# An LSTM with residual: the last 38 time steps with the hidden units in two halves

## The chip, the cores and the metric

The kernel runs on one core of a Trainium2 chip. A core has a matrix engine (TensorE, PE in the profile, with its weight loads as PEld), VectorE (DVE), ScalarE (ACT), GpSimd (POOL) and SyncE (SP), which here issues nearly all DMAs. The metric is the device time of one execution in microseconds, as the median of several runs.

## The reference, cut to what matters

```python
def lstm_forward(x, h0, Wx, Wh, b):            # x 32 x 512 x 512, all float32
    Hd = h0.shape[1]                           # 512
    xW = jnp.einsum('ntd,dg->ntg', x, Wx) + b  # Wx, Wh: 512 x 2048
    c0 = jnp.zeros_like(h0)
    def step(carry, xw_t):
        prev_h, prev_c = carry
        a = xw_t + prev_h @ Wh
        i = jax.nn.sigmoid(a[:, :Hd])
        f = jax.nn.sigmoid(a[:, Hd:2 * Hd])
        o = jax.nn.sigmoid(a[:, 2 * Hd:3 * Hd])
        g = jnp.tanh(a[:, 3 * Hd:])
        next_c = f * prev_c + i * g
        next_h = o * jnp.tanh(next_c)
        return ((next_h, next_c), next_h)
    (_, _), hs = jax.lax.scan(step, (h0, c0), jnp.swapaxes(xW, 0, 1))
    return jnp.swapaxes(hs, 0, 1)
return x + lstm_forward(x, cond_1024, L0_cond_Wx, L0_cond_Wh, L0_cond_b)
```

There are 32 sequences of 512 steps. Each step needs the h of the step before, so the 512 products h Wh come one after the other; the product x Wx has no such order.

## The kernel before, in words

**Layout.** The 128 partitions hold four groups j of 32 sequences: group j holds units 128 j to 128 j + 127 of each gate, and the 512 free columns are the four gates (i, f, g, o) of 128 units each. Every matmul has 32 stationary columns and writes 32 partitions, so that four of them, for the four j, use the array side by side. All is float32, and the profile shows each matmul as two.

**The loop.** The loop over k does one time step: `h_part(k)`, then the products of a *window* v = k + 4, then `cell(k)`. `h_part` (L667 to L678) adds h Wh to two PSUM banks that ScalarE has filled with the step's x Wx + b ("seeds", `seed_first` and `seed_last`, L656 to L662): first the 384 columns of i, f and g into bank `gates[t % 2]`, then the 128 columns of o into the other one. Consecutive steps so swap the banks. `cell` (L684 to L717) does two sigmoids, two tanhs, the sums and products on VectorE, and a transpose of 32 x 32 blocks that makes h the stationary operand `ht` of the next step. GpSimd adds x to it for the output (L710) and adds the bias to the x Wx of a coming step (L652).

**x Wx.** The first 40 steps and the last 16 (the tail, from END = 496) are multiplied plainly or nearly so. The 456 between them go by a fast matrix algorithm with 20 products per super-block of 24 steps, spread over the windows; a planner with due times (`push`, `run_due`) puts its sums on VectorE, its results go to DRAM and come back as `xw` two or three steps ahead. Each product of the fast algorithm occupies PE in windows w to w + 4 and is read out until w + 5; the last product of the last super-block begins at window 475.

**The tail's plain products.** `tail_products(v)` (L629 to L644) starts at window `FIRST_TAIL` = 481, which is step 477. From there on every window does two of 64 *pieces* (t, q): a quarter of the depth of one tail step's x Wx, all 512 columns, in 16 matmul rows. When the four pieces of a step are done, VectorE adds the bias (`keep_direct`, L620) into a free buffer (`tail_rooms`) that stays until its step seeds it. The six PSUM banks of the fast algorithm serve in turn (`tail_bank`). Two blocks of Wx, overwritten earlier, are loaded again into `raw_again` (L778 to L781, at windows 476 and 478).

**What sets the order.** Each engine runs its instructions in the program's order, which is written out by hand as above. All DMAs of this part stand in SP's queue in program order too, so a transfer that waits holds those behind it.

Of the kernel before, what the change touches and what calls it, by code (L numbers as in the profile page):

```python
# [9 lines left out]
F32 = mybir.dt.float32  # L10
AF = mybir.ActivationFunctionType
# [3 lines left out]
P = 128  # L15
B = 32
T = 512
NJ = 4
G = 4
IFG = 3 * P  # L20
ROW = 8
# [95 lines left out]
def begin(n):  # L117

    return 6 * (n // 5) + n % 5


class Job:
# [4 lines left out]
def kernel(  # L127
# [9 lines left out]
    nc = tc.nc  # L137
# [486 lines left out]
    tail_rooms, whole = [], []  # L624

    def tail_bank(t):
        return (*pps, *accs, p5)[t % 6]

    def tail_products(v):  # L629
        if v == FIRST_TAIL:  # L630
            tail_rooms.extend(node.rearrange("p t e b -> p (t e b)") for node in node_free)
            for f in free[: (TAIL - len(tail_rooms) + 1) // 2]:
                tail_rooms.extend([f[:, 0], f[:, 1]])
            assert len(tail_rooms) >= TAIL
        if v < FIRST_TAIL:
# [8 lines left out]
        del pieces[:2]  # L644

    def load_xw(t):
        xw[t] = upool.tile([P, G * P], F32, name=f"xw_{t}", tag="xw", bufs=4)
# [5 lines left out]

    def seed_first(t):  # L656
        if t < T:
            nc.scalar.copy(gates[t % 2][:, 0:IFG], xw[t][:, 0:IFG])  # L658

    def seed_last(t):  # L660
        if t < T:
# [5 lines left out]
    def h_part(t):  # L667
        for g, cols in ((gates[t % 2], slice(0, IFG)), (gates[(t + 1) % 2], slice(IFG, G * P))):
            for k in range(NJ):
                for j in range(NJ):  # L670
                    nc.tensor.matmul(  # L671
                        g[j * B : (j + 1) * B, cols],
                        state["ht"][:, k, :],
                        wh_sb[:, k, j, cols],
                        start=False,
                        stop=True,
                        skip_group_check=True,
                    )  # L678

    def x_last():  # L680
        state["x"] = work.tile([P, P], F32, name="x_last")
# [2 lines left out]
    def cell(t):  # L684
        n, tt = divmod(t, ROW)
        s = work.tile([P, G, P], F32, name=f"s_{t}", tag="s")
        fc = work.tile([P, P], F32, name=f"fc_{t}", tag="fc")
        c = work.tile([P, P], F32, name=f"c_{t}", tag="c", bufs=2)
        tc_t, h = ig, fc
        ht = work.tile([P, NJ, B], F32, name=f"ht_{t}", tag="ht", bufs=3)  # L690

        g = gates[t % 2].rearrange("p (g u) -> p g u", u=P)
        o = gates[(t + 1) % 2].rearrange("p (g u) -> p g u", u=P)[:, 3]
        nc.scalar.activation(s[:, 0:2], g[:, 0:2], AF.Sigmoid)  # L694
        nc.scalar.activation(s[:, 2], g[:, 2], AF.Tanh)
        nc.scalar.activation(s[:, 3], o, AF.Sigmoid)  # L696
        nc.vector.tensor_mul(fc, s[:, 1], state["c"])  # L697
        nc.vector.tensor_mul(ig, s[:, 0], s[:, 2])  # L698
        nc.vector.tensor_add(c, fc, ig)  # L699
        nc.scalar.activation(tc_t, c, AF.Tanh)  # L700
        nc.vector.tensor_mul(h, s[:, 3], tc_t)  # L701
        if t == T - 1:
            nc.vector.tensor_add(tc_t, h, state["x"])
            nc.sync.dma_start(out=out[n][:, tt * P : (tt + 1) * P], in_=tc_t)
            return
        nc.vector.transpose(ht.rearrange("p q b -> p (q b)"), h)  # L706
        state["c"], state["ht"] = c, ht
        if tt % 2 == 0:
            state["oc"] = opool.tile([P, 2, NJ, B], F32, name=f"oc_{t}", tag="oc")
        (nc.gpsimd if t < T - 3 else nc.vector).tensor_add(state["oc"][:, tt % 2], xr[t][:, tt % 2], ht)  # L710
# [55 lines left out]
    def fetch(v):  # L766

        job = jobs.get(v + 2)
        if job and job.w >= START and len(B_OF[job.kind[1]]) > 1:
            job.ring = [rpool.tile([P, 3, C], F32, name=f"wa_{job.w}", tag="wa", bufs=3), None]  # L770
            nc.sync.dma_start(out=job.ring[0].rearrange("p n c -> p (n c)"), in_=kept[job.kind[1]][0])
        job = jobs.get(v)
        if job and job.w >= START and len(B_OF[job.kind[1]]) > 1:
            job.ring[1] = rpool.tile([P, 4, C], F32, name=f"wb_{job.w}", tag="wb", bufs=4)
            nc.sync.dma_start(out=job.ring[1].rearrange("p n c -> p (n c)"), in_=kept[job.kind[1]][1])
        if v in (FIRST_TAIL - 10, FIRST_TAIL - 8):
            load_row(END // ROW + (v - FIRST_TAIL + 10) // 2)
        if v in (FIRST_TAIL - 5, FIRST_TAIL - 3):  # L778
            i = [i for i in range(8) if i not in single][(v - FIRST_TAIL + 5) // 2]
            raw[i] = rpool.tile([P, 4, C], F32, name=f"raw_again_{i}", tag="wb", bufs=4)  # L780
            nc.sync.dma_start(out=raw[i].rearrange("p n c -> p (n c)"), in_=wx[i])  # L781
        sb, rest = divmod(v + 6 - START, PER)
        if v + 6 in UNIT_AT[2 * NJ :: NJ]:
            load_row(3 + UNIT_AT[2 * NJ :: NJ].index(v + 6))
        if rest < MO and 0 <= sb < NSB:
            load_row(HEAD // ROW + MO * sb + (0, 2, 1)[rest])

    with tc.manual_schedule():
# [45 lines left out]
        for k in range(T):  # L834
            if k % 2 == 0 and k + 2 < T:
                load_residual(k + 2)
            if 2 * 4 - 3 <= k and k + 3 < END:
                load_xw(k + 3)
            h_part(k)
            if 2 * 4 - 2 <= k and k + 2 < END:  # L840
                add_bias(k + 2)
            for m, v in enumerate(windows_of(k)):
                if v == START:
                    assert len(due) == 0 or due[0][0] >= START
                    free.extend(t.rearrange("p (h n) c -> p h (n c)", h=2) for t in others)
                    free.extend(spool.tile([P, 2, 2 * C], F32, name=f"slot_h{i}", tag="sums", bufs=2) for i in range(2))
                announce(v)
                room = ROOM if v >= START - 4 else HEAD_ROOM
                run_due(v, room - evacuate(v, room))
                products(v)  # L850
                tail_products(v)
                fetch(v)
                if k == T - 2:
                    x_last()
                if m == 0:
                    cell(k)
                    seed_first(k + 2)
                    seed_last(k + 1)
                for op in prepare(v + 1):
                    op()  # L860
# [52 lines left out]
```

## Time and profile before

| | |
|---|---|
| median of 3 runs | 3124.21 us (3122.48 to 3124.5) |
| the profiled execution | 3124.46 us, span 3122.6 us |
| granted clock, mean | 0.999 |
| PE busy | 3108.1 us, 100% of the span |
| DVE, ACT, POOL busy | 2253.4, 1606.1, 1068.6 us |
| h Wh on PE (L671) | 32704 matmul rows, mean 380 ns |

The profile is one execution on the chip. A row of a timeline gives the start (us from the span's start), the time, the engine, the line of the kernel, the operation, and out<-in with shapes; rows of one kind that follow each other closely are merged (x64), and in brackets stands the engine's idle time before it with what ended it. The end of a matmul is modelled and rows overlap, so the pace of PE is read from start to start. A row of a group has the busy time, the mean ns of one, and the idle time before it. The chain of waits follows the work back from the last instruction.

### The profile page before, as it was taken

What the parts mean: (1) busy time and instruction counts of PE and PEld (TensorE: products, weight loads), DVE (VectorE), ACT (ScalarE), POOL (GpSimd) and SP (SyncE); (2) the same over time, 40 slices, a digit from 0 to 9 for tenths busy, and PEclk for the clock granted to TensorE, in tenths of its full rate; (3) what the DMA queues carried; (4) which work ended last, traced back from release to release, by engine and by line L of the source; (5) the groups of instructions that cost most, each with busy time, mean ns of one, the idle gap of its engine ahead of it and who ended that gap; (6) DMA issues with size and microseconds to landing.
All of it is one profiled execution on the core that took longest, in us unless ns stands there. A gap on an engine that the chain in (4) does not pass through costs nothing.

```text
span 3122.6 us, 133354 instructions
## 1 busy us (share of the span) xinstructions
PE 3108.1 (100%) x56632; PEld 2022.5 (65%) x56632; DVE 2253.4 (72%) x6107; ACT 1606.1 (51%) x4842; POOL 1068.6 (34%) x1001
## 2 busy tenths in 40 slices
PE   9999999999999999999999999999999999999999
PEld 5666666666666666666666666666666666666554
DVE  6557777777777777777777777777777777777533
ACT  2455555555555555555555555555555555555433
POOL 0223333333333333333333333333333333333320
PEclk9999999999999999999999999999999999999999
DMA  6656666767575766657676757667576767576410
GB/s 246 212 161 209 211 220 189 232 206 234 193 239 174 240 205 207 228 189 231 201 230 205 232 178 234 201 217 231 186 230 197 231 205 237 177 234 202 155 56 26
DMA packets 316084, 631.63 MB, mean 202 GB/s; under 512 B 41952, under 2 KB 107744, under 8 KB 314976
## 3 DMA queue, kind: packets, MB, share of 16 engines
q1 hardware_dynamic: 315344, 623.09, 61.7%
q8 instruction: 446, 7.31, 1.0%
q14 instruction: 150, 1.23, 0.1%
q10 hardware_dynamic: 144, 0.01, 0.0%
HBM read 448.60 MB, written 174.33 MB: 199 GB/s over the span
## 4 chain that ended last, share of the span: by engine, by line
PE 99%; DVE 0%; ACT 0%; DMA 0%; issue 0%; SPq 0%; DVEq 0%
PE gates L671 57%; PE acc L413 17%; PE pp L413 17%; PE p L413 6%; PE pp L604 1%; PE gates L604 1%; PE acc L604 1%; PE p L604 0%; DMA raw_sb<-in_L_cond_Wx_dram 0%; DVE ig L698 0%; DVE c L699 0%; ACT s L694 0%; ACT ig L700 0%; DVE fc L701 0%; DVE fc L697 0%
## 5 line engine op out<-in xcount | busy, mean ns | idle before, releaser
L671 PE MATMUL gates<-wh_sb,ht 128*32 128x384 f32 x32704 | 1873.6, 380 | 7.9 <-DVE ht L706 7.8
L671 PEld LDWEIGHTS gates<-wh_sb,ht 128*32 128x32 f32 x32704 | 1131.9, 110 | 770.9 <-issue 667.2
L710 POOL TENSOR_TENSOR oc<-xr,ht 128x128 f32<-128x128 f32 x509 | 445.2, 875 | 1925.3 <-DVE ht L706 1908.2
L652 POOL TENSOR_TENSOR xw<-xw,bias_sb 128x512 f32<-128x512 f32 x488 | 638.3, 1308 | 110.6 <-DMA xw<-xw 66.6
L694 ACT ACTIVATE s<-gates 128x256 f32<-128x256 f32 x512 | 197.4, 386 | 785.6 <-PE gates L671 785.6
L697 DVE TENSOR_TENSOR fc<-s,c 128x128 f32<-128x128 f32 x511 | 154.0, 301 | 482.7 <-ACT s L694 482.4
L455 ACT COPY pp<-pu 128x512 f32<-128x512 f32 x396 | 237.0, 599 | 153.5 <-DVE slot L563 81.3
L701 DVE TENSOR_TENSOR fc<-s,ig 128x128 f32<-128x128 f32 x512 | 150.4, 294 | 192.6 <-ACT ig L700 192.6
L413 PE MATMUL pp<-wb,node 128*32 128x256 f32 x3040 | 243.9, 379 | 0.0
L696 ACT ACTIVATE s<-gates 128x128 f32<-128x128 f32 x512 | 142.3, 278 | 183.8 <-PE gates L671 183.6
L658 ACT COPY gates<-xw 128x384 f32<-128x384 f32 x492 | 232.7, 473 | 5.9 <-DVE node L620 4.6
L706 DVE STREAM_TRANSPOSE ht<-fc 128x128 f32<-128x128 f32 x511 | 159.1, 311 | 53.4
L456 ACT COPY pp<-acc 128x256 f32<-128x256 f32 x396 | 142.1, 359 | 97.3 <-DVE slot L563 42.0
L700 ACT ACTIVATE ig<-c 128x128 f32<-128x128 f32 x512 | 158.7, 310 | 64.5 <-DVE c L699 31.8
L457 DVE TENSOR_TENSOR pp<-acc,p 128x256 f32<-128x256 f32 x396 | 167.7, 423 | 32.8 <-ACT pp L456 31.0
L449 DVE TENSOR_TENSOR pu<-acc,p 128x256 f32<-128x256 f32 x396 | 163.6, 413 | 25.3 <-ACT p L446 16.4
L446 ACT COPY p<-p 128x256 f32<-128x256 f32 x396 | 149.7, 378 | 48.0 <-PE p L413 42.1
L413 PE MATMUL pp<-wb,s 128*32 128x256 f32 x2128 | 170.8, 379 | 0.0
L413 PE MATMUL acc<-wb,s 128*32 128x256 f32 x2128 | 170.7, 379 | 0.0
L413 PE MATMUL p<-wa,s 128*32 128x256 f32 x2128 | 170.7, 379 | 0.0
L413 PE MATMUL acc<-wa,s 128*32 128x256 f32 x2128 | 170.7, 379 | 0.0
L699 DVE TENSOR_TENSOR c<-fc,ig 128x128 f32<-128x128 f32 x512 | 151.5, 296 | 17.8
(187 smaller groups left out, 4127.9 us busy)
## 6 DMA issues: line engine op xcount, KB each, us to landing
wb<-keep_b SPq DMA_DIRECT2D x266, 512.0 KB, 5.4
xw<-xw SPq DMA_DIRECT2D x488, 256.0 KB, 4.1
wa<-keep_a SPq DMA_DIRECT2D x266, 384.0 KB, 4.6
xw<-slot SPq DMA_DIRECT2D x528, 128.0 KB, 3.3
xr<-in_x_dram SPq DMA_DIRECT2D x256, 128.0 KB, 3.2
out_dram<-oc SPq DMA_DIRECT2D x255, 128.0 KB, 2.6
row<-in_x_dram SPq DMA_DIRECT2D x63, 512.0 KB, 6.2
xw<-slot_h SPq DMA_DIRECT2D x180, 128.0 KB, 3.6
```

The source lines that it names most:

```text
L413: nc.tensor.matmul(dst[t * B : (t + 1) * B], a[:, t], w, start=s in (1, 5) and m == 0, stop=True, skip_group_check=True,)
L449: nc.vector.tensor_add(job.pu[:, 1], job.acc, job.p5)
L455: nc.scalar.copy(job.pp[0], job.pu)
L457: nc.vector.tensor_add(job.pp[1][:, 1], job.acc, job.p5)
L652: nc.gpsimd.tensor_add(xw[t], xw[t], bias_sb)
L658: nc.scalar.copy(gates[t % 2][:, 0:IFG], xw[t][:, 0:IFG])
L671: nc.tensor.matmul(g[j * B : (j + 1) * B, cols], state["ht"][:, k, :], wh_sb[:, k, j, cols], start=False, stop=True, skip_group_check=True,)
L694: nc.scalar.activation(s[:, 0:2], g[:, 0:2], AF.Sigmoid)
L697: nc.vector.tensor_mul(fc, s[:, 1], state["c"])
L700: nc.scalar.activation(tc_t, c, AF.Tanh)
L706: nc.vector.transpose(ht.rearrange("p q b -> p (q b)"), h)
L710: (nc.gpsimd if t < T - 3 else nc.vector).tensor_add(state["oc"][:, tt % 2], xr[t][:, tt % 2], ht)
```

## The change

From step `HALVES` = 474 on (38 steps), the 128 units of each partition group are split into two halves of 64. Half m has its own PSUM bank for all steps, and uses 256 columns of it (four gates of 64 units).

- `h_halves` takes the place of `h_part`: four blocks of two depths k and one half m, in the order (k 0 and 1, half 0), (k 0 and 1, half 1), (k 2 and 3, half 0), (k 2 and 3, half 1). Depths 0 and 1 need only the first half of h, depths 2 and 3 only the second. The moving operand is cut: four runs of 64 columns.
- `cell_halves` does the cell twice, on 64 units each time, first all of half 0 and then all of half 1. The three gate activations of a half are followed by its seed for the next step, into the bank that they have just read.
- The tail's plain products start at window 478 (step 474) in place of 481, with one piece in the first window and two in each later one. Their banks are taken in another order, and a buffer is taken for each tail step when it is needed, in place of all at once.
- The second load of `raw_again` is issued at window 477 in place of 478; the rows of x and the first one stay at their windows.
- The last step adds x to each half and stores both with one DMA. `put_step` is the old end of `cell`, unchanged.

```diff
+LAST = START + PER * (NSB - 1) + begin(R - 1)
+HALVES = LAST + 3 - 4
...
-    FIRST_TAIL = START + PER * (NSB - 1) + begin(R - 1) + 6
-    tail_rooms, whole = [], []
-    def tail_bank(t):
-        return (*pps, *accs, p5)[t % 6]
+    whole = []
+    tail_banks = [p5, accs[1 - LAST % 2], accs[LAST % 2], *pps]
+    def tail_room():
+        if not node_free:
+            f = free.pop(0)
+            return f[:, 0]
+        return node_free.pop(0).rearrange("p t e b -> p (t e b)")
     def tail_products(v):
-        if v == FIRST_TAIL:
-            tail_rooms.extend(node.rearrange("p t e b -> p (t e b)") for node in node_free)
-            for f in free[: (TAIL - len(tail_rooms) + 1) // 2]:
-                tail_rooms.extend([f[:, 0], f[:, 1]])
-            assert len(tail_rooms) >= TAIL
-        if v < FIRST_TAIL:
+        if v < LAST + 3:
             return
         for t in whole:
-            keep_direct(t, tail_bank(t), tail_rooms[t - END])
+            keep_direct(t, tail_banks[(t - END) % 6], tail_room())
         whole.clear()
-        for t, q in pieces[:2]:
-            direct(t, tail_bank(t), (q,))
+        for t, q in pieces[: 1 if v == LAST + 3 else 2]:
+            direct(t, tail_banks[(t - END) % 6], (q,))
...
+    halves = gates[HALVES % 2], gates[(HALVES + 1) % 2]
+    HP = P // 2
+    def half(a, m):
+        return a.rearrange("p (g u) -> p g u", u=P)[:, :, m * HP : (m + 1) * HP]
+    def bank_half(m):
+        return halves[m][:, 0 : G * HP].rearrange("p (g u) -> p g u", u=HP)
+    def seed_half(t, m):
+        if t < T:
+            nc.scalar.copy(bank_half(m), half(xw[t], m))
     def seed_first(t):
-        if t < T:
+        if t == HALVES:
+            seed_half(t, 0)
+        elif t < HALVES:
             nc.scalar.copy(gates[t % 2][:, 0:IFG], xw[t][:, 0:IFG])
...
+    def h_halves(t):
+        for ks in ((0, 1), (2, 3)):
+            for m in range(2):
+                for k in ks:
+                    for j in range(NJ):
+                        nc.tensor.matmul(
+                            bank_half(m)[j * B : (j + 1) * B],
+                            state["ht"][:, k, :],
+                            half(wh_sb[:, k, j], m),
+                            start=False,
+                            stop=True,
+                            skip_group_check=True,
+                        )
...
+    def cell_halves(t):
+        us = [slice(m * HP, (m + 1) * HP) for m in range(2)]
+        def gates_of(m):
+            g, u = bank_half(m), us[m]
+            nc.scalar.activation(s[:, 0:2, u], g[:, 0:2], AF.Sigmoid)
+            nc.scalar.activation(s[:, 2, u], g[:, 2], AF.Tanh)
+            nc.scalar.activation(s[:, 3, u], g[:, 3], AF.Sigmoid)
+        def sums_of(m):
+            u = us[m]
+            nc.vector.tensor_mul(fc[:, u], s[:, 1, u], state["c"][:, u])
+            nc.vector.tensor_mul(ig[:, u], s[:, 0, u], s[:, 2, u])
+            nc.vector.tensor_add(c[:, u], fc[:, u], ig[:, u])
+        def end_of(m):
+            u = us[m]
+            nc.vector.tensor_mul(fc[:, u], s[:, 3, u], ig[:, u])
+            if t == T - 1:
+                nc.vector.tensor_add(ig[:, u], fc[:, u], state["x"][:, u])
+            else:
+                nc.vector.transpose(ht[:, 2 * m : 2 * m + 2].rearrange("p q b -> p (q b)"), fc[:, u])
+        gates_of(0)
+        seed_half(t + 1, 0)
+        sums_of(0)
+        nc.scalar.activation(ig[:, us[0]], c[:, us[0]], AF.Tanh)
+        end_of(0)
+        gates_of(1)
+        seed_half(t + 1, 1)
+        sums_of(1)
+        nc.scalar.activation(ig[:, us[1]], c[:, us[1]], AF.Tanh)
+        end_of(1)
...
-        if v in (FIRST_TAIL - 10, FIRST_TAIL - 8):
-            load_row(END // ROW + (v - FIRST_TAIL + 10) // 2)
-        if v in (FIRST_TAIL - 5, FIRST_TAIL - 3):
+        if v in (LAST - 4, LAST - 2):
+            load_row(END // ROW + (v - LAST + 4) // 2)
+        if v in (LAST + 1, LAST + 2):
...
-            h_part(k)
+            (h_part if k < HALVES else h_halves)(k)
...
-                    cell(k)
+                    (cell if k < HALVES else cell_halves)(k)
```

More of the change, by code (lines that the diff above doesn't have):

```diff
@@ L652, in add_bias @@
         nc.gpsimd.tensor_add(xw[t], xw[t], bias_sb)
+    halves = gates[HALVES % 2], gates[(HALVES + 1) % 2]
[7 more added lines that the diff above has]
+            nc.scalar.copy(bank_half(m), half(xw[t], m))
     def seed_first(t):
-        if t < T:
+        if t == HALVES:
+            seed_half(t, 0)
+        elif t < HALVES:
             nc.scalar.copy(gates[t % 2][:, 0:IFG], xw[t][:, 0:IFG])
     def seed_last(t):
-        if t < T:
+        if t == HALVES:
+            seed_half(t, 1)
+        elif t < HALVES:
             nc.scalar.copy(gates[(t + 1) % 2][:, IFG:], xw[t][:, IFG:])
@@ L701, in cell, with put_step @@
         nc.vector.tensor_mul(h, s[:, 3], tc_t)
[L702 to L705, printed above, removed]
         nc.vector.transpose(ht.rearrange("p q b -> p (q b)"), h)
         state["c"], state["ht"] = c, ht
+        put_step(t)
+    def cell_halves(t):
+        n, tt = divmod(t, ROW)
+        s = work.tile([P, G, P], F32, name=f"s_{t}", tag="s")
+        fc = work.tile([P, P], F32, name=f"fc_{t}", tag="fc")
+        c = work.tile([P, P], F32, name=f"c_{t}", tag="c", bufs=2)
+        ht = work.tile([P, NJ, B], F32, name=f"ht_{t}", tag="ht", bufs=3) if t < T - 1 else None
+        us = [slice(m * HP, (m + 1) * HP) for m in range(2)]
[26 more added lines that the diff above has]
+        end_of(1)
+        if t == T - 1:
+            nc.sync.dma_start(out=out[n][:, tt * P : (tt + 1) * P], in_=ig)
+            return
+        state["c"], state["ht"] = c, ht
+        put_step(t)
+    def put_step(t):
+        n, tt = divmod(t, ROW)
+        ht = state["ht"]
         if tt % 2 == 0:
@@ L775, in fetch @@
             nc.sync.dma_start(out=job.ring[1].rearrange("p n c -> p (n c)"), in_=kept[job.kind[1]][1])
-        if v in (FIRST_TAIL - 10, FIRST_TAIL - 8):
-            load_row(END // ROW + (v - FIRST_TAIL + 10) // 2)
-        if v in (FIRST_TAIL - 5, FIRST_TAIL - 3):
-            i = [i for i in range(8) if i not in single][(v - FIRST_TAIL + 5) // 2]
+        if v in (LAST - 4, LAST - 2):
+            load_row(END // ROW + (v - LAST + 4) // 2)
+        if v in (LAST + 1, LAST + 2):
+            i = [i for i in range(8) if i not in single][v - LAST - 1]
             raw[i] = rpool.tile([P, 4, C], F32, name=f"raw_again_{i}", tag="wb", bufs=4)
```

2 lines of the change are left out of this document (1 added, 1 removed).

## The prediction

> **What bounds the kernel now.** I read the stretches of the last 200 us first, then PE's timeline in them, then one late step on all engines, then Pool. In what follows "step k" is one time step; its h Wh starts with the first L671 of the step.
>
> ```profile
> span 3122.6 us, 133354 instructions
> ...
> 2915.80:2932.70 16.90, 12.73 (x232) 7.37 (x229) 11.01 (x24) 6.31 (x20) 6.93 (x7) 0.99 0.74 221
> 2932.70:2939.50 6.80, 6.80 (x81) 2.81 (x82) 1.39 (x5) 1.79 (x6) 1.71 (x3) 0.78 0.24 77
> 2939.50:3099.10 159.60, 159.56 (x2408) 78.97 (x2408) 52.03 (x165) 53.52 (x180) 33.59 (x47) 1.00 0.16 52
> 3099.10:3122.60 23.50, 16.19 (x272) 8.78 (x271) 7.03 (x24) 6.02 (x21) 0.74 (x2) 1.00 0.08 24
> ```
>
> Columns: stretch, its length, busy time of PE, weight load, DVE, ACT, POOL, then granted clock, DMA share, GB/s. PE lacks 4.2 us of work in the first stretch, runs at a clock of 0.78 in the second, looks full in the third, and idles again in the last. PE's timeline names the steps (474, 475, 476, 477, 478 start with an L671 row each):
>
> ```profile
> 2904.44 3.66 PE L671 MATMUL gates<-wh_sb,ht 128*32 128x384 f32 x64
> 2907.89 0.64 PE L413 MATMUL pp<-wb,node 128*32 128x256 f32 x8
> 2908.32 0.64 PE L413 MATMUL acc<-t,s 128*32 128x256 f32 x8
> ...
> 2915.80 3.66 PE L671 MATMUL gates<-wh_sb,ht 128*32 128x384 f32 x64
> 2920.11 0.64 PE L413 MATMUL pp<-wb,s 128*32 128x256 f32 x8
> 2921.11 3.66 PE L671 MATMUL gates<-wh_sb,ht 128*32 128x384 f32 x64 [0.36 <-DVE ht L706]
> 2924.56 0.64 PE L413 MATMUL pp<-wb,node 128*32 128x256 f32 x8
> 2926.42 3.66 PE L671 MATMUL gates<-wh_sb,ht 128*32 128x384 f32 x64 [1.22 <-DVE ht L706]
> ...
> 2939.50 3.66 PE L671 MATMUL gates<-wh_sb,ht 128*32 128x384 f32 x64
> ```
>
> The first three rows are the price list of a PE that never waits: 3.45 us for h Wh (2904.44 to 2907.89), 0.43 for a group of products. A plain piece is two such groups by length, 0.86. Steps 474 to 477 run out of products, and each next L671 waits for the transposed h. The third stretch looks full but is not. By the chain:
>
> ```profile
> 2932.68 5.16 PE gates L671 x64
> ...
> 2939.55 3.60 PE gates L671 x64
> ...
> 3099.06 3.59 PE gates L671 x64
> ```
>
> Thirty steps, 478 to 508, take 159.51 us, 5.317 each; their work is 3.45 + 2 x 0.86 = 5.17. Step 477 pays 5.16 for what costs 3.60 later. Here is what sets the 5.317:
>
> ```profile
> 2944.84 3.66 PE L671 MATMUL gates<-wh_sb,ht 128*32 128x384 f32 x64
> 2947.68 0.38 ACT L694 ACTIVATE s<-gates 128x256 f32<-128x256 f32 x1 [3.08 <-PE gates L671]
> 2948.10 0.29 DVE L697 TENSOR_TENSOR fc<-s,c 128x128 f32<-128x128 f32 x1 [2.48 <-ACT s L694]
> 2948.31 0.29 DVE L698 TENSOR_TENSOR ig<-s 128x128 f32<-128x128 f32 x1
> 2948.63 0.29 DVE L699 TENSOR_TENSOR c<-fc,ig 128x128 f32<-128x128 f32 x1
> 2948.95 0.31 ACT L700 ACTIVATE ig<-c 128x128 f32<-128x128 f32 x1
> 2949.30 0.29 DVE L701 TENSOR_TENSOR fc<-s,ig 128x128 f32<-128x128 f32 x1 [0.37 <-ACT ig L700]
> 2949.69 0.31 DVE L706 STREAM_TRANSPOSE ht<-fc 128x128 f32<-128x128 f32 x1
> 2950.15 3.66 PE L671 MATMUL gates<-wh_sb,ht 128*32 128x384 f32 x64
> ```
>
> 2.84 us from the start of h Wh to the first activation (the i, f, g columns), then 2.47 us of cell until h is back on PE. Behind the i, f, g columns PE has only the o columns (0.86) and two pieces (1.72), and falls 0.15 short each step. The cell bounds the tail, by a little with products and by nearly 2 us without.
>
> **The change, part by part.** (a) *Half a cell.* The trace has no 64-column instruction; neighbours in size give the slope:
>
> ```profile
> L694 ACT ACTIVATE s<-gates 128x256 f32<-128x256 f32 x512 | 197.4, 386 | 785.6 <-PE gates L671 785.6
> L696 ACT ACTIVATE s<-gates 128x128 f32<-128x128 f32 x512 | 142.3, 278 | 183.8 <-PE gates L671 183.6
> L456 ACT COPY pp<-acc 128x256 f32<-128x256 f32 x396 | 142.1, 359 | 97.3 <-DVE slot L563 42.0
> L457 DVE TENSOR_TENSOR pp<-acc,p 128x256 f32<-128x256 f32 x396 | 167.7, 423 | 32.8 <-ACT pp L456 31.0
> L699 DVE TENSOR_TENSOR c<-fc,ig 128x128 f32<-128x128 f32 x512 | 151.5, 296 | 17.8
> ```
>
> ACT: 0.108 us per 128 columns; DVE: 0.127. So a half saves 0.108 on the two-gate sigmoid, 0.054 on the tanh of c, about 0.064 on each DVE operation. Along the rows of the step above, from activation to PE: 0.42 + 0.21 + 0.32 + 0.32 + 0.35 + 0.39 + 0.46 = 2.47; minus 0.108 + 5 x 0.064 + 0.054 gives **1.99 us** for the first half. Bounds: nothing saved but the 0.108 (2.36), or everything in proportion (1.24); I take the slope, as both engines show one.
>
> The second half follows in the same queues. Its sigmoid stands behind the first half's tanh of c (at 0.97) and starts at 1.12; its DVE operations stand behind the first transpose and start at 1.76; with the same spacings its h is on PE at **3.44 us**. The seeds of the next step move into these queues as well, two copies of 256 columns. The first must end before the first tanh of c is due: sigmoid of o done near 0.52 (estimate, three short activations one behind the other), copy 0.36 by the 256-column row, end 0.91 against 0.97. Six hundredths of slack: a copy that is longer goes straight onto the path.
>
> (b) *h Wh in four blocks of 0.86.* 64 matmuls as before, same columns. The first cell starts after three blocks, 2.84, as now (three of four quarters, as 384 of 512 columns). The built program lets block 1 wait for the first transpose alone and block 3 for the second, and block 2 for its seed (near 2.1). After the first activation PE has block 4 and products: free at 0.86 - 0.27 + 1.72 = 2.31 (0.27: 2.84 less 2.57 of columns). The first h is there at 1.99, the second at 3.44 against 2.31 + 1.72 = 4.03. So with two pieces the step becomes PE's own 5.17. Operands cut into runs of 64 columns are the unknown: no row has one. I take no cost, because eight half-width matmuls (the 0.43 row above) and four full-width ones take the same 0.43 per group, so more beginnings are hidden; the other end is open (first rival).
>
> (c) *Products from step 474.* Their weights must be there:
>
> ```profile
> 2905.83 0.38 SPq L781 DMA_DIRECT2D raw_again<-in_L_cond_Wx_dram  x1
> ...
> 2910.74 1.75 SPq L473 DMA_DIRECT2D xw<-slot_h  x4
> ...
> 2923.03 0.37 SPq L781 DMA_DIRECT2D raw_again<-in_L_cond_Wx_dram  x1
> ```
>
> The first load is issued 14.7 us before the first piece (2920.5, below). The second moves one window up on SP, ahead of an output, a residual row, a load of xw and two groups of stores, to the end of the stores of 2910.74, near 2912.5, and is wanted at 2926; what it passes is issued 0.5 us later, and what stood behind it 0.5 earlier. DVE takes one bias addition for every four pieces, as before, now behind the second transpose, where it is idle; in front of a first half its 0.69 us would come onto the path.
>
> The sum, against the profiled execution (3124.46 us with 3122.6 span; the median is 3124.21):
>
> Steps 474 to 477: before 2915.80 to 2939.50, 23.70. After: 474 is 3.45 + 3 x 0.43 + 0.86 = 5.60; 475 is 3.45 + 0.43 + 1.72 = 5.60; 476 and 477 are 5.17: 21.54. **Gain 2.16**, and seven pieces are done instead of two.
> Steps 478 to 505: 28 x (5.317 - 5.17). **Gain 4.1.**
> Step 506 has one piece, 507 to 511 none. From the start of 506 to the next start and on, the cell bounds: 2.84 + 1.99 = 4.83. Before, 506 starts at 2939.55 + 28 x 5.317 = 3088.43 and the last cell at 3117.77 (below): 29.34. After: 5 x 4.83 + 2.84 = 26.99. **Gain 2.35.**
>
> ```profile
> 3117.77 0.39 ACT L694 ACTIVATE s<-gates 128x256 f32<-128x256 f32 x1 [3.56 <-PE gates L671]
> 3119.71 0.29 DVE L703 TENSOR_TENSOR ig<-fc,x_last 128x128 f32<-128x128 f32 x1
> ```
>
> Last cell: 2.23 us before. After, the second half ends it: addition of x at about 2.88, done 3.1. **Loss 0.87**; the output DMA is the same.
> Together 2.16 + 4.1 + 2.35 - 0.87 = 7.74: **3116.7 us**, 0.25% less.
>
> [...] The second stretch lost about 1.5 us to the clock (6.8 x 0.22), and PE's longest idle time before it is 2.59 us. [...] By the row the loss goes with the gaps; were the slow step another thing and to stay, the sum would be 3118.2, the third rival's case.
>
> **The rivals.** *1. The cut operand slows PE (slower).* Each of 38 steps reads Wh in runs of 64. At 0.20 us a step (7.74 / 38), 6% of 3.45, the gain is gone; at 15% (0.52 us) the time is 3136.4. For it: no row excludes it. Against it: the two equal 0.43 groups.
>
> *2. Pool holds the cell.*
>
> ```profile
> 2930.03 1.27 POOL L652 TENSOR_TENSOR xw<-xw,bias_sb 128x512 f32<-128x512 f32 x1 [3.21 <-DMA xw<-xw]
> 2930.21 1.24 DVE L699 TENSOR_TENSOR c<-fc,ig 128x128 f32<-128x128 f32 x1
> 2944.77 0.46 POOL L710 TENSOR_TENSOR oc<-xr,ht 128x128 f32<-128x128 f32 x1 [3.66 <-DVE ht L706]
> 2945.19 1.28 POOL L652 TENSOR_TENSOR xw<-xw,bias_sb 128x512 f32<-128x512 f32 x1
> ```
>
> The DVE addition that began inside Pool's bias addition took 0.95 us more. [...] Until step 493 Pool adds out and bias behind the whole transposed h, 1.70 us from the start of the one to the end of the other, so from about 3.4 to 5.1 after; the next half cell's first DVE operation is at 5.17 + 0.31 = 5.48. It misses by under 0.4 us. If Pool comes later than that, a hold of 0.95 less the 0.32 that PE has in hand (1.99 against 2.31) is 0.63 in each of 20 steps: 3129.3.
>
> *3. The first steps stay unfilled*, because a hold or a store's wait keeps the clock or the 2 us: 3118 to 3119.
>
> *4. Halves cost more than the slope says.* With nothing saved but the 0.108 the first h comes at 2.36, past 2.31: 31 x 0.05 + 5 x 0.37 + 0.6 (the last cell's second half) = 4.0 less gain, 3120.7; halfway, where the pieces still cover it, 5 x 0.19 + 0.3, 3118.0.
>
> *5. No overlap* (block 1 waits for the whole h): a step of 3.44 + 2.84 = 6.28 us instead of 5.317, 38 times: 3161. The waits of the built program speak against it.
>
> **How the numbers follow.** Likeliest, as summed: 0.62, 3115 to 3118.2. Rival 3: 0.12. Rival 4: 0.10. Rival 2: 0.08. Rival 1: 0.06. Rival 5: 0.02. The range takes in the first three cases: 3114.5 to 3121.5. A measurement of this kernel tells 0.2% (6.2 us, below 3118) from no change; its three runs spread over 2 us. Faster: nearly all of the likeliest and a little of 3 and 4, 0.60. Slower: rivals 1, 5 and half of 2, 0.12. Same: 0.28.
>
> **What would show it.** Right: steps of 5.17 us from 476 on with h Wh at 3.45 and no clock below 0.99; steps of 4.83 from 506 on; the last cell 3.1 us long; 64-column DVE operations of 0.23 and ACT of 0.22. Wrong: an h Wh over 3.6; DVE operations over 1 us inside Pool's additions; idle time of PE ahead of block 3 (second half late) or of block 1 in steps with pieces.

## The result, and the profile after

The changed kernel takes **3116.23 us** (median, 3115.69 to 3117.25) against 3124.24 us of the kernel before on the same chip (3122.33 to 3125.61): 8.0 us less, a ratio of 0.9975 with a 95% interval of 0.9966 to 0.9985. The profiled execution took 3116.83 us. The forecast was 3116.7.

First the page of the changed kernel, then the stretches of its last 200 us: stretch, its length, busy time of PE, weight load, DVE, ACT and POOL with the number of instructions, then granted clock, DMA share and GB/s.

```profile
span 3115.0 us, 133680 instructions
...
PE 3103.1 (100%) x56632; PEld 2044.2 (66%) x56632; DVE 2278.1 (73%) x6297; ACT 1620.4 (52%) x4994; POOL 1066.7 (34%) x1001
```

```profile
2916.00:2932.40 16.40, 16.40 (x268) 10.42 (x268) 11.42 (x37) 7.18 (x31) 6.81 (x6) 1.00 0.66 194
2932.40:2937.60 5.20, 5.20 (x85) 3.15 (x81) 2.60 (x12) 2.17 (x10) 1.70 (x2) 1.00 0.34 111
2937.60:3082.30 144.70, 144.70 (x2244) 88.08 (x2240) 64.12 (x295) 60.54 (x280) 32.72 (x44) 1.00 0.17 55
3082.30:3115.00 32.70, 22.88 (x396) 14.60 (x388) 13.94 (x67) 12.51 (x59) 1.83 (x4) 0.96 0.09 26
```

The stretch that had 4.2 us of idle PE is full (16.40 of 16.40), and the one at a clock of 0.78 runs at 1.00; the 0.96 of the last one comes from the 4.9 us behind PE's last matmul (0.72 there), the steps before it run at 1.00. The third was "full" before too, so its busy time says nothing; the starts of h Wh (L706 now) do. PE's timeline of the changed kernel at steps 474 to 478, two late steps, and 506, 507, 508 and 511:

```profile
2916.05 3.66 PE L706 MATMUL gates<-wh_sb,ht 128*32 128x256 f32 x64
...
2921.65 3.66 PE L706 MATMUL gates<-wh_sb,ht 128*32 128x256 f32 x64
...
2927.25 3.66 PE L706 MATMUL gates<-wh_sb,ht 128*32 128x256 f32 x64
...
2932.42 3.66 PE L706 MATMUL gates<-wh_sb,ht 128*32 128x256 f32 x64
2935.88 0.59 PE L608 MATMUL acc<-raw_again,row 128*32 128x512 f32 x1
...
2937.59 3.66 PE L706 MATMUL gates<-wh_sb,ht 128*32 128x256 f32 x64
...
2947.93 3.66 PE L706 MATMUL gates<-wh_sb,ht 128*32 128x256 f32 x64
...
2953.10 3.66 PE L706 MATMUL gates<-wh_sb,ht 128*32 128x256 f32 x64
...
3082.35 3.66 PE L706 MATMUL gates<-wh_sb,ht 128*32 128x256 f32 x64
...
3087.19 3.66 PE L706 MATMUL gates<-wh_sb,ht 128*32 128x256 f32 x64 [0.31 <-DVE fc L757]
...
3092.01 3.66 PE L706 MATMUL gates<-wh_sb,ht 128*32 128x256 f32 x64 [1.17 <-DVE fc L757]
...
3106.55 3.66 PE L706 MATMUL gates<-wh_sb,ht 128*32 128x256 f32 x64 [1.19 <-DVE fc L757]
```

Steps 474 to 477 take 21.54 us (2916.05 to 2937.59), the 28 steps 478 to 505 take 144.76 (5.17 each, to 3082.35), and from 507 on PE idles again for the cell: 4.82 to 4.86 a step. The h Wh of step 477 ends in issue after 3.46 us (2932.42 to 2935.88), against 3.45 uncut.

One late step of the changed kernel on ACT, from the first activation of half 0:

```profile
2950.79 0.28 ACT L751 ACTIVATE s<-gates 128x128 f32<-128x128 f32 x1 [2.55 <-PE gates L706]
...
2951.38 0.38 ACT L671 COPY gates<-xw 128x256 f32<-128x256 f32 x1
2951.76 0.26 ACT L772 ACTIVATE ig<-c 128x64 f32<-128x64 f32 x1
```

And on DVE and POOL:

```profile
2951.10 0.23 DVE L757 TENSOR_TENSOR fc<-s,c 128x64 f32<-128x64 f32 x1 [2.33 <-ACT s L751]
2951.24 0.22 DVE L758 TENSOR_TENSOR ig<-s 128x64 f32<-128x64 f32 x1
2951.50 0.23 DVE L759 TENSOR_TENSOR c<-fc,ig 128x64 f32<-128x64 f32 x1
...
2953.70 0.24 DVE L767 STREAM_TRANSPOSE ht<-fc 128x64 f32<-128x64 f32 x1
...
2948.85 0.46 POOL L790 TENSOR_TENSOR oc<-xr,ht 128x128 f32<-128x128 f32 x1 [3.23 <-DVE ht L767]
2949.27 1.28 POOL L654 TENSOR_TENSOR xw<-xw,bias_sb 128x512 f32<-128x512 f32 x1
```

Pool's bias addition ends at 2950.55, DVE's first operation of the half cell starts at 2951.10: 0.55 us between them in this step. Over the late steps with such an addition (from step 477 on) the distance is between 0.30 and 0.55, as Pool sometimes starts later.

### The profile page after: what moved, and what is told of

Read it like the earlier page. It is cut to its first block, busy times and chain, and to the rows that moved or that the text cites. A ratio compares the mean times of both kernels' runs of the same rounds, so it can differ in the third digit from the quotient of the medians.

```text
span 3115.0 us, 133680 instructions
## 1 busy us (share of the span) xinstructions
PE 3103.1 (100%) x56632; PEld 2044.2 (66%) x56632; DVE 2278.1 (73%) x6297; ACT 1620.4 (52%) x4994; POOL 1066.7 (34%) x1001
## 4 chain that ended last, share of the span: by engine, by line
PE 99%; DVE 0%; DMA 0%; ACT 0%; issue 0%; SPq 0%; DVEq 0%
PE gates L692 53%; PE pp L417 17%; PE acc L417 17%; PE p L417 6%; PE gates L706 4%; PE pp L608 1%; PE gates L608 1%; PE acc L608 1%; PE p L608 0%; DMA raw_sb<-in_L_cond_Wx_dram 0%; DVE ig L733 0%; DVE fc L757 0%; ACT s L751 0%; DVE c L759 0%; DVE fc L763 0%
## 5 line engine op out<-in xcount | busy, mean ns | idle before, releaser
L692 PE MATMUL gates<-wh_sb,ht 128*32 128x384 f32 (+1 forms) x30272 | 1733.1, 379 | 0.4 <-DVE ht L737 0.3
L692 PEld LDWEIGHTS gates<-wh_sb,ht 128*32 128x32 f32 x30272 | 1053.7, 110 | 682.0 <-issue 615.4
L729 ACT ACTIVATE s<-gates 128x256 f32<-128x256 f32 x474 | 182.6, 385 | 671.2 <-PE gates L692 671.2
L732 DVE TENSOR_TENSOR fc<-s,c 128x128 f32<-128x128 f32 x473 | 141.4, 299 | 369.0 <-ACT s L729 368.6
L736 DVE TENSOR_TENSOR fc<-s,ig 128x128 f32<-128x128 f32 x474 | 138.5, 292 | 178.4 <-ACT ig L735 178.4
L677 ACT COPY gates<-xw 128x384 f32<-128x384 f32 x470 | 222.2, 473 | 4.8 <-DVE node L624 4.6
L731 ACT ACTIVATE s<-gates 128x128 f32<-128x128 f32 x474 | 131.7, 278 | 169.8 <-PE gates L692 169.2
L737 DVE STREAM_TRANSPOSE ht<-fc 128x128 f32<-128x128 f32 x474 | 147.6, 311 | 49.5
L735 ACT ACTIVATE ig<-c 128x128 f32<-128x128 f32 x474 | 147.1, 310 | 59.5 <-DVE c L734 28.0
L446 ACT COPY pu<-acc 128x256 f32<-128x256 f32 x396 | 146.5, 370 | 28.0 <-PE acc L417 28.0
```

The source lines that it names most:

```text
L692: nc.tensor.matmul(g[j * B : (j + 1) * B, cols], state["ht"][:, k, :], wh_sb[:, k, j, cols], start=False, stop=True, skip_group_check=True,)
```

## The experiments

The table puts together what the traces below gave. Each figure is the distance between starts of h Wh; the last column runs from the start of step 474 to the end of the span, which leaves out differences in the 2900 us before. Single steps that left their row (at most 0.35 us longer each, such as 5.42 once in before and 5.66 once with the early pieces alone) are not in the columns, but are in the last one.

```
                     474   475   476   477   478-505     506-510     474 to end
before               5.32  5.31  6.26  6.82  5.34, 5.31  5.31        206.78
after                5.60  5.60  5.17  5.17  5.17        4.83-4.86   199.00
halves alone         4.89  5.38  4.83  5.17  5.17        5.17; 4.83  198.67  (5.17 to 508)
early pieces alone   5.61  5.60  5.32  5.31  5.31        5.31        205.29
spread               4.88  5.39  4.82  5.17  5.17        4.83-4.86   197.72
spread, last cell    4.89  5.37  4.83  5.17  5.17        4.83-4.86   197.29
Pool four times      5.60  6.14  5.95  5.95  5.95; 5.17  4.83        213.92  (5.95 to 493)
Pool twice           5.60  5.60  5.17  5.17  5.17        4.83-4.86   198.99
one more on DVE      5.60  5.60  5.17  5.17  5.17        5.09-5.12   200.68
two more on DVE      5.60  5.70  5.34  5.34  5.34        5.34-5.38   207.88
six more on DVE      6.45  6.93  6.39  6.39  6.39        6.39; 7.92  249.16
```

**The two parts, each alone.** First the halves without the earlier pieces:

```diff
-        if v < LAST + 3:
+        if v < LAST + 6:
...
-        for t, q in pieces[: 1 if v == LAST + 3 else 2]:
+        for t, q in pieces[:2]:
```

> The changed kernel with the halves from step 474 kept, and the plain pieces moved back to window 481 (step 477), two a window, as in the kernel before. Theory A (the sum by steps, worked on from the trace of the changed kernel): a half-cell step takes the longer of its PE work and 4.83 us, so an early piece is only free where it fits under 4.83; steps 474, 475 and 476 without pieces take 4.83 each (work 4.74, 3.88, 3.45), then 32 steps of 5.17 and 509, 510 at 4.83. From the start of step 474 to the end 198.0 us against 198.95 with the early pieces: 0.9 us faster than the changed kernel, near 3115.3 us, and the granted clock stays at 1.00, as in the changed kernel's last steps with 1.2 us of idle PE each. Theory B (the early pieces earn their 2 us as the prediction booked them, by keeping PE busy and its clock up): the clock falls in steps 476 to 478 as in the kernel before, the step after them takes over 5 us on h Wh alone, and the time is 1.5 to 3 us above the changed kernel, 3118 to 3119.

Measured: 3115.63 us, ratio 0.9975 (0.9965 to 0.9985). Then the earlier pieces with the old cell (the addition of x in the last step goes back into it as well, not shown):

```diff
-HALVES = LAST + 3 - 4
+HALVES = T
```

> The kernel's old whole cell and old two-block h Wh in all steps, with the plain pieces from step 474 as in the changed kernel. Theory A: a whole-cell step takes the longer of its PE work and 5.317 us; steps 474 and 475 take 5.60, the 35 steps 476 to 510 5.317, and the gain over the kernel before is only the lost clock and the held step, 206.8 - 205.0 = 1.8 us, so about 3122.4 us; granted clock at 1.00 throughout. Then the two parts do not add up: 1.8 alone and 8.8 alone (halves) against 7.9 together. Theory B (parts add): the early pieces are worth the gain that the halves alone leave, several us.

Measured: 3122.59 us, 0.9996 (0.9987 to 1.0005). By its interval the second run is not told from the kernel before; its trace is. From the start of step 474 the halves alone gain 8.1 us (206.78 - 198.67), the pieces alone 1.5, both together 7.8. The 1.5 is the size of what the slow clock cost in the traced execution of before (see *The clock* below), and the granted clock is 1.00 in both these runs. So the parts do not add up: the early pieces fill idle time that the halves take away as well, and on top of the halves they are worth -0.3. PE's timeline of the kernel with the halves alone shows why:

```profile
2915.60 3.66 PE L706 MATMUL gates<-wh_sb,ht 128*32 128x256 f32 x64
...
2920.49 3.66 PE L706 MATMUL gates<-wh_sb,ht 128*32 128x256 f32 x64
...
2925.87 3.66 PE L706 MATMUL gates<-wh_sb,ht 128*32 128x256 f32 x64 [1.29 <-DVE fc L757]
...
2930.69 3.66 PE L706 MATMUL gates<-wh_sb,ht 128*32 128x256 f32 x64 [1.16 <-DVE fc L757]
```

Without pieces a step costs the chain's 4.83, with two it costs 5.17, with two and a product 5.60. In these traces a second piece in a step costs 0.34; five pieces moved ahead cost 1.27 there (21.54 against 20.27 for steps 474 to 477) and save 3 x 0.34 = 1.0 in 506 to 508.

Step 475 took 5.38 here where the chain should have given 4.83; without that the halves alone would have come near the 198.0 us expected. DVE and POOL of that step, halves alone:

```profile
2923.30 0.68 DVE L567 TENSOR_TENSOR slot_h<-pp,raw_sb 128x512 f32<-128x512 f32 x1
2923.90 0.53 DVE L757 TENSOR_TENSOR fc<-s,c 128x64 f32<-128x64 f32 x1
...
2923.06 1.28 POOL L654 TENSOR_TENSOR xw<-xw,bias_sb 128x512 f32<-128x512 f32 x1
```

The planner's last sums stand ahead of the half cell on DVE until 2923.98, so its first operation starts 0.25 us late (0.56 instead of 0.31 behind the first activation of 2923.34), and is then held until Pool's addition ends at 2924.34: 0.53 instead of 0.23. Together that is the 0.55. In the changed kernel step 474 takes 5.60 instead of 4.89, so that the sums (to 2924.43) and Pool's addition (to 2924.79) are over when the half cell's first DVE operation of step 475 starts at 2924.82. It takes 0.23: the hold is missed by 0.03 us, and the 5.60 us of PE work in that step would have covered it.

**The pieces spread.** One piece in each of steps 475 and 476, two in each of 477 to 505, one in each of 506 to 509, so that fewer steps pay for a second one:

```diff
-        if v < LAST + 3:
+        if v < LAST + 4:
...
+        n = 1 if v < LAST + 6 or v >= LAST + 35 else 2
-        for t, q in pieces[: 1 if v == LAST + 3 else 2]:
+        for t, q in pieces[:n]:
```

> The changed kernel with the same 64 pieces spread to where a half-cell step has room: none in step 474, one each in 475 and 476, two each in 477 to 505, one each in 506 to 509. Theory A: a step with one piece (4.31 of work) still takes 4.83, so 29 steps of 5.17 and 8 of 4.83 stand between 474 and 510: 196.9 us from the start of 474 to the end, 2.0 us less than the changed kernel, near 3114.2 us, the least of all versions here. Theory B (more idle PE per step, so the clock or a late bias addition takes it back): no gain, 3116 us or more.

Measured: 3115.45 us, 0.9973 (0.9962 to 0.9984); 197.72 us from the start of 474, 1.28 less than the changed kernel. The expected 196.9 was missed by 0.8, of which 0.56 is step 475 (5.39 instead of 4.83), where DVE and Pool stand in the way as above.

**Is it Pool's margin that holds?** Pool's output addition repeated, so that its bias addition ends later; first four times, later twice:

```diff
-        (nc.gpsimd if t < T - 3 else nc.vector).tensor_add(state["oc"][:, tt % 2], xr[t][:, tt % 2], ht)
+        for _ in range(4 if HALVES <= t < END - 2 else 1):
+            (nc.gpsimd if t < T - 3 else nc.vector).tensor_add(state["oc"][:, tt % 2], xr[t][:, tt % 2], ht)
```

> The changed kernel; in steps 474 to 493 Pool's output addition is done four times in place of once (the same sum written again), 3 x 0.42 = 1.26 us more of Pool in each, and nothing else. In the changed kernel Pool ends its bias addition 0.55 us before the next half cell's first VectorE operation. Theory A (a VectorE operation with two SBUF inputs that begins inside a Pool operation is held until that ends): the first operation of the half cell is held by 0.7 to 1.1 us, h of the first half comes later than PE's 0.36 us in hand, and these 20 steps take 5.5 to 5.9 us in place of 5.17: 7 to 14 us more, 3123 to 3131 us. Theory B (the two share and only Pool is slower, or Pool is beside the path): 5.17 us a step, 3116.2 us.

> The changed kernel; Pool's output addition of steps 474 to 493 is done twice in place of once, 0.42 us more of Pool in each. Theory A (a lock with 0.55 us in hand): Pool ends 0.13 us before the next half cell's first VectorE operation, steps stay at 5.17 and the time at 3116.2 us within 1 us. Theory B (every microsecond of Pool costs VectorE something): 20 x 0.42 = 8 us more, 3124 us.

Measured with four: 3131.51 us, 1.0024 (1.0015 to 1.0034), so 7.3 us slower than before. With two: 3116.38 us, 0.9975 (0.9966 to 0.9984), as the changed kernel. POOL and DVE of a late step with four:

```profile
2970.36 2.07 POOL L791 TENSOR_TENSOR oc<-xr,ht 128x128 f32<-128x128 f32 x4 [2.64 <-DVE ht L767]
2972.39 1.28 POOL L654 TENSOR_TENSOR xw<-xw,bias_sb 128x512 f32<-128x512 f32 x1
...
2972.27 0.24 DVE L757 TENSOR_TENSOR fc<-s,c 128x64 f32<-128x64 f32 x1 [1.41 <-ACT s L751]
2972.43 1.32 DVE L758 TENSOR_TENSOR ig<-s 128x64 f32<-128x64 f32 x1
```

And with two:

```profile
2950.19 1.28 POOL L654 TENSOR_TENSOR xw<-xw,bias_sb 128x512 f32<-128x512 f32 x1
...
2951.48 0.22 DVE L757 TENSOR_TENSOR fc<-s,c 128x64 f32<-128x64 f32 x1 [2.32 <-ACT s L751]
```

With four, the bias addition starts 2.03 us after the output addition instead of 0.42, and DVE's second operation, begun inside it, takes 1.32 us instead of 0.22 and ends 0.08 after it. Of these 1.10 us PE hides 0.32 to 0.34, and the step is 5.95 instead of 5.17 in each of the 18 steps that have the hold from 476 on. With two, it starts 0.53 later (0.42 was expected), ends at 2951.47, and DVE starts at 2951.48, 0.31 behind its activation as before: the margin of 0.55 is used up and nothing is lost. So a delay of 1.61 us on an engine that is busy for a third of the span costs 15 us over the changed kernel.

**How much slack the chain has.** The product by o of the first half, on DVE, was repeated two, six, and one more time; the repeats wait for one another and lie on the way to the first transpose:

```diff
-            nc.vector.tensor_mul(fc[:, u], s[:, 3, u], ig[:, u])
+            for _ in range(3 if m == 0 else 1):   # 7 and 2 in the others
+                nc.vector.tensor_mul(fc[:, u], s[:, 3, u], ig[:, u])
```

> The changed kernel; the product o tanh(c) of the first half is done three times in place of once (the same result again), which puts about 2 x 0.15 = 0.3 us on the first half's chain in each of the 38 steps. Theory A (in steps with pieces PE is the bound and the first half has 0.36 us in hand; only the last five steps hang on it): steps with two pieces stay at 5.17 to 5.20, the steps from 506 on grow from 4.83 to about 5.13, 1.5 us in all, 3117.7 us. Theory B (the cell still sets every step): 38 x 0.3 = 11 us more, 3127 us.

> As the run with three products, with seven: six more, about 0.9 us on the first half's chain (the second half stands behind it and comes later by as much, against 0.6 us in hand). Theory A: past the 0.36 us in hand the rest shows one for one: steps with two pieces 5.17 + 0.5 to 0.55 = 5.7, the last ones 5.7: 31 x 0.53 + 5 x 0.9 = 21 us more, 3137 us. Theory B (PE stays the bound): 3118 us. Theory C (nothing in hand): 38 x 0.9 = 34 us more, 3150 us.

> The changed kernel; the product o tanh(c) of the first half is done twice. The runs with two and six more showed that each repeat costs 0.26 us on the chain, and steps of the longer of 5.17 and 4.83 plus the repeats. Theory A (0.34 us in hand in a step with two pieces): one repeat of 0.26 is not seen there, steps stay at 5.17, and the last five grow to 5.09: 5 x 0.26 = 1.3 us more than the changed kernel, 3117.5 us. Theory B (nothing in hand, the earlier runs only grew with the repeats): 37 x 0.26 = 9.6 us more, 3126 us.

Measured: one more 3118.31 us (0.9984, 0.9975 to 0.9993), two more 3125.27 (1.0003, 0.9994 to 1.0013), six more 3166.62 (1.0135, 1.012 to 1.015). DVE's timeline, the row of one step each, with one, with two and with six more:

```profile
3000.34 0.48 DVE L764 TENSOR_TENSOR fc<-s,ig 128x64 f32<-128x64 f32 x2 [0.32 <-ACT ig L773]
```

```profile
2990.78 0.74 DVE L764 TENSOR_TENSOR fc<-s,ig 128x64 f32<-128x64 f32 x3 [0.32 <-ACT ig L773]
```

```profile
2997.02 1.78 DVE L764 TENSOR_TENSOR fc<-s,ig 128x64 f32<-128x64 f32 x7 [0.32 <-ACT ig L773]
```

A repeat costs 0.25 to 0.26 us, where my expectations for two and six went by 0.15. With the measured price the chain is 4.83 + 0.26 = 5.09 with one, 4.83 + 0.51 = 5.34 with two and 4.83 + 6 x 0.26 = 6.39 with six; PE's work is 5.17. Each step came out at the longer of the two: 5.17 with pieces and 5.09 without, 5.34, 6.39. So the numbers expected of the theories were off for two and six, by the size of the repeat; the rule that a step is the longer of the two holds at four chain lengths, the changed kernel's among them. With one more, the trace is 1.68 us longer than the changed kernel's from the start of 474 (200.68 against 199.00): 5 x 0.26 in the steps without pieces, 0.26 in the last cell, and one step of 5.31.

The run with six more also shows the clock. PE's timeline of its last steps, and stretches of 3.41 us from there, a length explained under *The clock* (columns as above):

```profile
3133.82 3.66 PE L706 MATMUL gates<-wh_sb,ht 128*32 128x256 f32 x64 [2.73 <-DVE fc L757]
3140.20 3.66 PE L706 MATMUL gates<-wh_sb,ht 128*32 128x256 f32 x64 [2.73 <-DVE fc L757]
3146.63 5.16 PE L706 MATMUL gates<-wh_sb,ht 128*32 128x256 f32 x64 [2.76 <-DVE fc L757]
3154.55 3.66 PE L706 MATMUL gates<-wh_sb,ht 128*32 128x256 f32 x64 [2.76 <-DVE fc L757]
```

```profile
3136.07:3139.48 3.41, 1.41 (x28) 0.69 (x20) 1.94 (x9) 1.91 (x9) 0.00 (x0) 1.00 0.24 77
...
3142.89:3146.30 3.41, 0.98 (x20) 0.38 (x12) 2.23 (x11) 1.91 (x9) 0.00 (x0) 1.00 0.00 0
3146.30:3149.72 3.42, 3.09 (x32) 1.71 (x36) 1.63 (x8) 0.26 (x1) 0.00 (x0) 0.50 0.11 38
3149.72:3153.13 3.41, 2.07 (x40) 1.01 (x32) 1.38 (x7) 1.91 (x9) 0.00 (x0) 1.00 0.00 0
3153.13:3156.55 3.42, 2.00 (x40) 1.50 (x44) 2.26 (x11) 0.26 (x1) 0.00 (x0) 1.00 0.02 5
```

**The last cell, and the whole again.** On top of the spread pieces, the last step does the gates of both halves, then both sums, and then the two ends, so that no half waits behind the other's long chain:

```diff
         gates_of(0)
+        if t == T - 1:
+            gates_of(1)
+            for m in range(2):
+                sums_of(m)
+            for m in range(2):
+                nc.scalar.activation(ig[:, us[m]], c[:, us[m]], AF.Tanh)
+                end_of(m)
+            nc.sync.dma_start(out=out[n][:, tt * P : (tt + 1) * P], in_=ig)
+            return
```

> The spread pieces, and in the last step alone both halves' gate activations and sums stand ahead of the first tanh of c in their queues. The second half's sigmoid then starts with the end of block 4 (0.86 us after the first) in place of 1.13, and its VectorE sums no longer stand behind the first half's end. By the durations of the changed kernel the last cell takes 2.6 us from its first activation to the end of the addition of x, in place of 3.08: 0.5 us less than the spread kernel, 197.2 us from the start of step 474 to the end, about 3115.0 us. If the queues' order is not what the last cell hangs on: 3.08 us and 3115.4.

> The changed kernel itself, beside the others on the same chip, as the mark for differences of about 1 us: 3116.2 us, 199.0 us from the start of step 474 to the end.

Measured: 3114.70 us (3114.28 to 3115.41), ratio 0.9971 (0.9959 to 0.9982); the changed kernel on the same chip 3116.47 (3115.78 to 3117.73), 0.9978 (0.9969 to 0.9987). The first activation and the last addition of the last cell, by the timelines of ACT and DVE, here and then in the changed kernel:

```profile
3107.70 0.28 ACT L752 ACTIVATE s<-gates 128x128 f32<-128x128 f32 x1 [2.21 <-PE gates L707]
...
3110.13 0.23 DVE L766 TENSOR_TENSOR ig<-fc,x_last 128x64 f32<-128x64 f32 x1
```

```profile
3109.41 0.28 ACT L751 ACTIVATE s<-gates 128x128 f32<-128x128 f32 x1 [2.21 <-PE gates L706]
...
3112.26 0.23 DVE L765 TENSOR_TENSOR ig<-fc,x_last 128x64 f32<-128x64 f32 x1
```

2.66 us to the end of the last row instead of 3.08. In the changed kernel's second run all steps came out as in the first. By its median this version is the fastest of all that ran: 1.8 us under the changed kernel, with no run of the one as long as any of the other, and 9.0 under the kernel before. Against the spread pieces alone (3115.45, runs that overlap with these) only the traces tell it: 197.29 against 197.72 us.

## Why the prediction was right, and where it was not

*The four terms.* Steps 474 to 477: 21.54 us forecast, 21.54 measured. Steps 478 to 505: 5.17 each, as forecast. Step 506 to the last cell: 26.99 forecast, 27.06 measured (a gain of 2.34: in the trace of before step 506 starts at 3088.37, where the prediction had worked out 3088.43). The last cell: 3.1 forecast, 3.08 measured. From the start of 474 the gain is 7.78 against 7.74. The span itself fell by about 7.5, as step 474 begins 0.25 later (2916.05 against 2915.80); the prediction gave that no term.

*What the first term was credited to.* Its size is right and its reading is not: "Gain 2.16, and seven pieces are done instead of two" reads as the earlier pieces' gain. The halves alone take those four steps in 20.27 us, and the pieces give 0.3 back over the whole. The shorter chain alone cuts the idle time there (1.29 and 1.16 us are left before steps 476 and 477, where before had 1.22 and 2.59), and the clock stays at 1.00; the pieces alone fill the idle time and keep the clock as well, for 1.5 us. The prediction's own numbers could have told it: it had 4.83 as the step without pieces and 5.17 with two, so a second piece of a step had a price of 0.34, and it counted that price only at the end, in the gain of 506 to 511. That the first term came out to the hundredth is therefore right arithmetic on steps that PE's work bounds, and no sign that the pieces were worth it.

*The half cell.* 64-column operations on DVE take 0.22 to 0.23 in the first half (forecast 0.23; in the second the first of them takes 0.18, and the transposes take 0.24 to 0.25), on ACT 0.22 to 0.26 (forecast 0.22). The step without pieces is 4.83, so the first h is at 1.99 as forecast; the second transpose starts 2.91 after the first activation. The slack of 0.32 (2.31 less 1.99) is confirmed from both sides: 0.26 more on DVE is hidden, and of 0.51 more all but 0.34 shows (5.34 or 5.35 instead of 5.17). The copy of a seed was the thinnest place, and thinner than forecast: it ends at 0.97 after the first activation, not at 0.91, because it takes 0.38 and begins at 0.59. The tanh of c starts at 0.97, right behind it. The six hundredths were not there; nothing was lost, as c itself is ready at 0.94.

*The rivals.* The cut operand (1) costs nothing that shows: 3.46 against 3.45. Pool (2) holds DVE where it comes late (1.32 us instead of 0.22 with four output additions) and does not reach this kernel, but not by much: the margin is 0.55 in the step shown and 0.30 in the tightest of the late ones, so "under 0.4" was near, and it is 0.03 in step 475. The runs put the point from which it decides between 0.53 of delay (free) and 1.61 (0.78 us a step). The first steps are filled (3), the halves cost what the slope said (4), and the blocks overlap (5), as PE has no idle time from 474 to 506.

*The clock.* The second stretch's loss went with the gaps, as taken. The rows of two traces place a fall between matmuls. In the kernel before, the clock is at half from 2932.34 to 2935.75, 3.41 us, behind gaps of 0.36, 1.22 and 2.59 us, the last of them in this row of PE's timeline:

```profile
2932.68 5.16 PE L671 MATMUL gates<-wh_sb,ht 128*32 128x384 f32 x64 [2.59 <-DVE ht L706]
```

These are three stretches of 3.41 us, the one at half and those around it (length, PE's busy time and so on, granted clock third from the end):

```profile
2928.93:2932.34 3.41, 1.16 (x36) 0.81 (x28) 2.14 (x5) 1.65 (x6) 1.27 (x1) 1.00 0.80 241
2932.34:2935.75 3.41, 3.07 (x20) 1.14 (x24) 0.19 (x1) 0.13 (x1) 1.72 (x2) 0.50 0.55 176
2935.75:2939.17 3.42, 3.42 (x64) 1.69 (x56) 1.21 (x5) 1.67 (x6) 0.00 (x0) 1.00 0.02 5
```

With six more operations on DVE the clock is at half from 3146.30 to 3149.72, again 3.41 us, behind a gap of 2.76, while two gaps of 2.73 before it, and one of 2.76 after it, passed at full speed. What differs is where the gap lies when time is cut into stretches of 3.41 us from the moment of the fall. The gap behind which the clock fell (3143.87 to 3146.63) lies nearly whole in one stretch, which has 0.98 us of PE's work left, as the stretch ahead of the fall in before has 1.16. The gap after it (3151.79 to 3154.55) is shared by two stretches, with 2.07 and 2.00 us of work; of the gaps before it the worse leaves 1.41 in its stretch. So in these two traces the clock fell for 3.41 us behind a stretch of that length with 1.16 and 0.98 us of work, and not behind those with 1.41, 2.07 and 2.00. In the changed kernel it fell at 3112.28, behind PE's last matmul, and the stretch ahead of that (3108.87 to 3112.28) has 1.34. A limit near 1.4 us of 3.41 is an estimate from these figures: the ends of matmuls are modelled, and the profiled execution with one more operation has a clock of 0.999 too (3120.15 us, where its nine others, at 1.000, have a median of 3118.25), with no row here that places its fall. The gaps of 1.17 to 1.20 us between the changed kernel's last steps brought no fall; cut the same way, from the fall at 3112.28, each stretch from 3088.39 to 3108.87 has at least 2.21 us of work.

By this estimate a gap of 2.6 us would cost in some executions and not in others, and the record looks like it. Of the 29 executions of the kernel before that stand beside the last runs, 15 have a mean granted clock of 0.999 and a median of 3124.47 us, and 14 have 1.000 and 3122.83. One stretch of 3.41 us at half clock makes a mean of 0.99945, so the first kind fits one such stretch each, though only one of them was traced, and the record doesn't say where it lay in the others. The changed kernel's executions, 10 and then 11, are all at 1.000. The traced execution of before, from which the forecast was summed (3124.46), is of the first kind; against the second the changed kernel gains 6.4 us (3122.83 - 3116.47), and the early pieces alone nearly nothing (3122.59, against 3122.69 for the second kind beside that run). The time forecast does not hang on this, as the changed kernel has no such loss. The gain does: which kind the median of before falls to is chance, and that it came out at 8.0, close to the 7.74 summed from one traced execution, is in part luck.

## What to carry to other kernels

In a recurrence, write each step as the longer of two sums, the work that the engine has for the step and the chain from its result back to its start; cutting the state in halves shortens the second alone, and pays only as far as the first. Work put in to fill idle time is free only up to the longer sum, and what exceeds it is paid per step, so it belongs spread thinly over the steps with slack. Before shifting such a chain, measure the distance to the instructions of any engine that can hold it, as Pool held DVE here, in every step and not in one: a delay of 1.6 us on Pool turned 8 us gained into 7 lost.

## What the runs showed of the hardware

Each repeat of the 64-column DVE product, on the output of the one before, added 0.25 to 0.26 us (0.23 for one, 0.48 for two, 0.74 for three, 1.78 for seven), not the 0.15 that I had taken from the spacing of L757 and L758 (2951.10 to 2951.24), which do not wait for each other. Between matmuls the clock was at half for 3.41 us in the two traces whose rows are above (2932.34 in before, 3146.30 with six more operations), behind a stretch of that length in which PE had 1.16 and 0.98 us of work; with six more, the gap of 2.76 that lay across two such stretches (2.07 and 2.00 us of work) passed at 1.00. A DVE operation with both inputs in SBUF that began inside Pool's bias addition took 1.32 us instead of 0.22 in one step (with Pool four times) and 0.53 instead of 0.23 in another (halves alone), ending 0.08 to 0.09 us after Pool's each time. The planner's sum of 2923.30 (halves alone), with one input in a PSUM bank (`pp`), began inside the same addition of Pool and was over in 0.68 us, 0.36 ahead of it.
